# Softmax sums of a cross-attention: their reciprocals sent through memory and fetched back for all partitions, in place of a matrix product

## The chip, the cores and the metric

The kernel runs on one core of one Trainium2 chip. The metric is the device time of one execution in microseconds; the times shown are the median and the extremes of three runs. The profile is of one further execution.

## What is computed

The reference is one layer on x of shape (4, 256, 256), with a context of shape (4, 4096, 256): cross-attention, then a block that sends the top quarter of the tokens through a small attention and the rest through a state-space scan, then a mixture of eight experts. The change concerns the cross-attention:

```
q1 = split_heads(x1 @ Wq1)            # x1 = layernorm(x): 4 batches, 256 tokens, 8 heads of 64
k  = concat(x1 @ Wk1, ctx @ Wk2)      # 256 + 4096 = 4352 keys
v  = concat(x1 @ Wv1, ctx @ Wv2)
sim  = einsum('bihd,bjhd->bhij', q1, k) * 64 ** -0.5
attn = softmax(sim, axis=-1)
out  = einsum('bhij,bjhd->bihd', attn, v)
x = x + out.reshape(B, 256, 512) @ Wo + bo
```

The kernel leaves the probabilities unnormalised, sums them, and multiplies the output of each head and query by the reciprocal of its sum.

## The kernel before

**Tiling.** Heads go in pairs: a group G is one of 16 pairs of heads (4 batches by 4 pairs). A group's 256 queries are taken in 8 steps of 32 queries, so the stage has 128 steps, n = 8G + s, and two more to drain it. In a step the scores of 32 queries with all 4352 keys stand in PSUM (`su`), with four quarters of the keys on the four quarters of the partitions, once for each of the two heads. VectorE copies them to SBUF with their maximum (`copy_max`, L1401) and multiplies these maxima into `mq` (L1408); TensorE spreads the maxima (`stat`, L1413), and VectorE reduces them to `nb` (L1418). ScalarE takes the exponentials in place and leaves their sums in `ls` (`exps`, L1429). VectorE transposes them in blocks of 32 into `pt` (`turn`, L1438). When four steps are there, TensorE multiplies them with the values (`values`, L1447), in four pieces of a step with s = 1 or s = 5, into a PSUM tile `po`, which ScalarE copies to `ao` (`values_out`, L1484). Keys and values are made from the context, chunk by chunk, in the other steps (`k_chunk` L1328, `v_chunk` L1365).

**The sums of a group.** In the first step of the next group (s = 0), `sums(G - 1)` brings together the four quarters by a small product with `dm` (L1461), takes the reciprocals (`rl`, 64 partitions by 8 steps, L1466) and lays them out on diagonals (`dg`, L1468). In the step after it (s = 1), `spread(G - 1)` multiplies `dg` with the constant `pair` (L1475): in `psr`, a PSUM tile of 128 partitions by 256 queries, every partition then holds the reciprocals of its head. `normalize` (L1490) multiplies the two halves of `ao` with it, the first half in the middle of that step, the second one at its end, after `values_out` and the two transposes of the step.

**PSUM.** All short-lived products share the three banks of the pool `ps_m`: `bank(name)` takes one. `po` holds one through a step with s = 1, and `psr` another, from its product to the second `normalize`.

**Order.** The program is written out in order by hand. Between the pieces of a step, `slot(budget)` lets background generators issue the next piece of their work: the router, the small attention and the state-space scan of the batch before (`routed`, `attention`, `ssm_front`, `ssm_scan`). A planner's count `now[0]` grows by what each piece of TensorE work should take; a background piece is issued when its due time has come and its cost fits the budget. In the scan, `make` issues the decays (`da`, ScalarE, L731) and inputs (`db`, GpSimd, L736), `scan` the recurrence (VectorE, L743), and `output` the products (GpSimd, L749 and L751). Background transfers leave from SyncE's queue; small results also leave from ScalarE's. In the front of the background there are the tiles `pspr`, `projT`, `psas`, `psdt`, `ev` and `psat` (L556, L560, L419, L579, L586, L437), all of which but `projT` and `ev` are banks of `ps_m`. `bb` and `cb` (L714) are the scan's inputs, broadcast to all partitions from `bcd` in memory.

A last stage after the 130 steps computes the experts and the background of the last batch.

Of the kernel before, what the change touches and what calls it, by code (L numbers as in the profile page):

```python
# [8 lines left out]
F32 = mybir.dt.float32  # L9
AF = mybir.ActivationFunctionType  # L10
ALU = mybir.AluOpType
# [3 lines left out]
P = 128  # L15
B, T, D = 4, 256, 256
# [21 lines left out]
def bc(ap, axis, n):  # L38

    ap = ap.unsqueeze(axis)  # L40
    shape = list(ap.shape)
    shape[axis] = n
    return ap.to_broadcast(shape)
# [3 lines left out]
def perceiver_layer(ctx: ExitStack, tc: tile.TileContext, a: dict, out: bass.AP):  # L47
# [174 lines left out]
    def bank(name):  # L222
        return ps_m.tile([P, 512], F32, tag="m", name=name)
# [981 lines left out]
    with ExitStack() as s1:  # L1205
# [83 lines left out]
        def turn_x(b):  # L1289
# [9 lines left out]

        su = ps_s.tile([P, 5 * 512], F32, name="su")  # L1300


        pair = fin.tile([2 * 32, P], F32, name="pair")
        nc.vector.tensor_copy(
            pair.rearrange("p (j d) -> p j d", j=2), bc(quarter[: 2 * 32, 0:2, 0], 2, HD)
        )
        qzs = [fin.tile([P, 2, T], F32, name=f"qz{i}") for i in range(2)]
        for t in qzs:
            nc.gpsimd.memset(t, 0.0)
# [141 lines left out]
                        start=(k == 0), stop=(k == NJ - 1),  # L1451
                    )

        dgs, rss = {}, {}

        def sums(G):

            b, hp = divmod(G, NHP)
            ps = bank("psl")
            for j in range(2):  # L1460
                nc.tensor.matmul(  # L1461
                    ps[j * 32 : (j + 1) * 32, :8], dm, lss[b][:, hp, :, j],
                    start=True, stop=True,
                )
            rl = fin.tile([2 * 32, 8], F32, tag="rl", name="rl")
            nc.vector.reciprocal(rl, ps[: 2 * 32, :8])  # L1466
            dgs[G] = fin.tile([2 * 32, 8, 32], F32, tag="dg", name="dg")
            nc.vector.tensor_tensor(  # L1468
                dgs[G], bc(rl, 2, 32), bc(dm[: 2 * 32, :], 1, 8), ALU.mult
            )  # L1470

        def spread(G):

            rss[G] = bank("psr")[:, :T]
            nc.tensor.matmul(  # L1475
                rss[G], pair, dgs[G].rearrange("p s i -> p (s i)"), start=True, stop=True
            )

        def values_out(m):
# [39 lines left out]
        with tc.manual_schedule():  # L1519
            norms = {}  # L1520
            k_chunk(0, 0)
            wself[0] = load_self(0)
            nc.scalar.dma_start(out=bo_bc, in_=a["xbo"].partition_broadcast(P))
            for _ in norm(0):
                pass
            for g in range(1, NCH):
                k_chunk(0, g)
                if g == 4:
                    turn_x(0)
            k_self(0)  # L1530
            start(load_later())
            wv[0] = load_v(0)
            N = 8 * NG
            for n in range(N + 2):
                G, s = divmod(n, 8)
                new, old = n < N, 1 <= n <= N


                pieces, took = [], 1.75
                if s == 5 and G + 1 < NG:  # L1540
                    wv[G + 1] = load_v(G + 1)
                if s % 4 == 1:
                    m, took = n // 4 - 1, 1.95
                    if m >= 0:
                        pieces = [
                            lambda i=i: values(m, i, min(i + 9, NJ)) for i in range(0, NJ, 9)
                        ]
                elif 2 <= s <= 4 and G < NG:
                    pieces = [
                        lambda g=g: v_chunk(G, g) for g in range(3 * s - 6, 3 * s - 3)  # L1550
                    ]
                elif G + 1 < NG:
                    if s == 0:
                        wqk[G + 1] = load_qk(G + 1)
                        wself[G + 1] = load_self(G + 1)
                    pieces = {
                        0: [lambda g=g: k_chunk(G + 1, g) for g in range(3)],
                        6: [lambda g=g: k_chunk(G + 1, g) for g in range(3, 6)],
                        7: [lambda: k_self(G + 1)]
                        + [lambda g=g: k_chunk(G + 1, g) for g in range(6, 8)],  # L1560
                    }[s]


                tail = n >= N - 2

                def piece(i):
                    if i < len(pieces):
                        pieces[i]()
                    if i < len(pieces) or tail:
                        now[0] += took  # L1570

                if new:
                    scores(n)
                    now[0] += 2.1
                if old:
                    exps(n - 1)
                if new:
                    copy_max(n)
                piece(0)
                if s % 4 != 1:  # L1580
                    slot(1.3)
                    piece(1)
                    if old:
                        turn(n - 1, 0)
                    if new:
                        stat(n)
                        now[0] += 0.3
                    if s == 0 and n:
                        sums(G - 1)
                        now[0] += 0.2  # L1590
                    if old:
                        turn(n - 1, 1)
                    slot(1.3 if tail else 0.5)
                    piece(2)
                    slot(2.9)
                else:
                    last = s == 1 and G
                    if last:
                        spread(G - 1)
                        now[0] += 0.6  # L1600
                    slot(1.5)
                    piece(1)
                    if new:
                        stat(n)
                        now[0] += 0.3
                    slot(2.8)
                    if last:
                        normalize(m - 1)
                    if n == N + 1:

                        psx[B - 1] = bank("psx")
                        project(B - 1, 0, psx[B - 1], range(NHP))
                        add(B - 1, 0, psx[B - 1])
                        project(B - 1, 1, psx[B - 1], range(NHP - 1))
                    piece(2)
                    slot(1.5)
                    piece(3)
                    if n > 4:
                        values_out(m)
                    if old:  # L1620
                        turn(n - 1, 0)
                        turn(n - 1, 1)
                    if last:
                        normalize(m)
                        if m % 8 == 7:
                            start_first(finish_batch(m // 8))
                b = n // 32 + 1
                if b < B:
                    if n % 32 == 20:
                        norms[b] = norm(b)  # L1630
                    if n % 32 in (20, 22):
                        next(norms[b])
                    if n % 32 == 29:
                        turn_x(b)
# [301 lines left out]
```

## Time and profile before

| | us |
|---|---|
| median of 3 runs | 1546.52 |
| lowest, highest | 1540.41, 1550.73 |
| profiled execution, own time | 1548.97 |
| its span (first to last instruction) | 1547.3 |
| TensorE busy | 1458.9 (94%) |
| VectorE busy | 1059.8 (68%) |
| ScalarE busy | 757.8 (49%) |
| GpSimd busy | 410.6 (27%) |

The attention stage fills the first 1273 us of the span. In the profile, PE is TensorE, PEld its weight loads, DVE VectorE, ACT ScalarE, POOL GpSimd and SP SyncE; L and a number is a line of the kernel. Lines of the timeline give the start and the duration in us, the engine, the line, the operation, the tile written and those read, and in brackets how long the engine was idle before it and what it waited for. Groups of one tile give lowest, median and highest duration in ns, and the first and last start in us. A product of 32-bit floats shows as two passes, each with its weight load, so the counts of TensorE are doubled. Rows of DMA issues give the number, the size and the median time from issue to landing.

### The profile page before, as it was taken

The page shows a single profiled execution, that of the slowest core. Times are in us where ns is not written, and L with a number is a line of the kernel's source. Part 1 is how long each engine was busy: PE and PEld are TensorE (multiplying, and loading weights), DVE is VectorE, ACT ScalarE, POOL GpSimd, SP SyncE. Part 2 cuts the span into 40 slices and gives each one's busy share as a digit, 9 for nine tenths or more (in the row PEclk, how much of TensorE's full clock was granted, in tenths as well). Part 3 has the DMA queues.
Part 4 walks back from the last instruction along what each step waited for, and adds up shares of the span by engine and source line. Part 5 has one row for each costly group of instructions (what it writes and reads, how often), then busy time and mean ns, then how long its engine had stood idle before and what let it go on. Part 6 is the DMA issues. An engine that isn't in the chain of part 4 may idle for free.

```text
span 1547.3 us, 37278 instructions
## 1 busy us (share of the span) xinstructions
PE 1458.9 (94%) x15686; PEld 1039.8 (67%) x15686; DVE 1059.8 (68%) x1825; ACT 757.8 (49%) x1485; POOL 410.6 (27%) x464
## 2 busy tenths in 40 slices
PE   7999999999999999999999999999998968889799
PEld 3757667576666576775766666758575658778687
DVE  1666666666599976565899866757999554589553
ACT  3444454455566745454666453656654413544211
POOL 1000000000079950000599600003998010110100
PEclk9999999999999999999999999999999979999999
DMA  7455433514245434333554434244452206678471
GB/s 233 135 155 161 157 126 125 174 63 155 95 145 168 161 109 153 119 102 111 162 164 131 144 127 150 68 156 133 141 171 91 74 27 213 208 258 270 157 231 48
DMA packets 157768, 223.41 MB, mean 144 GB/s; under 512 B 14977, under 2 KB 76161, under 8 KB 157601
## 3 DMA queue, kind: packets, MB, share of 16 engines
q1 hardware_dynamic: 152368, 211.45, 42.1%
q10 hardware_dynamic: 3744, 5.51, 1.2%
q0 software_dynamic: 1488, 4.07, 0.9%
q8 instruction: 124, 2.03, 0.5%
q14 instruction: 44, 0.35, 0.1%
HBM read 216.56 MB, written 4.42 MB: 143 GB/s over the span
## 4 chain that ended last, share of the span: by engine, by line
PE 64%; POOL 15%; DVE 10%; DMA 4%; issue 4%; ACT 2%; SPq 0%; ACTq 0%; DVEq 0%; POOLq 0%
PE po L1447 12%; PE su L1381 11%; PE psv L1365 11%; PE psk L1328 9%; POOL y L751 5%; POOL db L736 5%; POOL db L749 5%; DVE sp L1401 3%; PE su L1389 2%; PE pg L1853 2%; PE pu L1853 2%; PE pde L1866 2%; PE p1b L1721 2%; DMA gateT<-in_gateT 2%; DVE db L743 1%
## 5 line engine op out<-in xcount | busy, mean ns | idle before, releaser
L1401 DVE TENSOR_SCALAR_CACHE_REDUCE sp<-su 128x1088 f32<-128x1088 f32 x256 | 318.8, 1281 | 182.0 <-PE su L1389 181.8
L1438 DVE STREAM_TRANSPOSE pt<-sp 128x1088 f32<-128x1088 f32 x256 | 328.0, 1295 | 58.7 <-PE po L1447 58.7
L1429 ACT ACTIVATE sp<-sp,nb 128x1088 f32<-128x1088 f32 x256 | 305.2, 1195 | 13.5 <-DVE nb L1418 13.3
L1447 PE MATMUL po<-pt,v 128*64 128x128 f32 x4352 | 262.9, 278 | 2.3 <-DVE pt L1438 1.3
L1381 PE MATMUL su<-kt,qz 64*32 64x512 f32 x4096 | 256.3, 609 | 4.4 <-DVE nb L1418 3.7
L1328 PE MATMUL psk<-ctx,wk 128*128 128x512 f32 x512 | 244.3, 611 | 10.5 <-DMA ctx<-in_ctxT 7.4
L1365 PE MATMUL psv<-wv,ctx 128*128 128x128 f32 x2048 | 250.8, 279 | 0.2 <-ACT da L731 0.2
L1447 PEld LDWEIGHTS po<-pt,v 128*64 128x64 f32 x4352 | 240.9, 139 | 13.9 <-issue 7.5
L1365 PEld LDWEIGHTS psv<-wv,ctx 128*128 128x128 f32 x2048 | 236.6, 192 | 6.4 <-issue 1.3
L1328 PEld LDWEIGHTS psk<-ctx,wk 128*128 128x128 f32 x512 | 91.3, 191 | 94.8 <-issue 84.4
L1316 ACT COPY kt<-psk 128x512 f32<-128x512 f32 x128 | 74.6, 584 | 158.2 <-PE psk L1328 157.9
L1381 PEld LDWEIGHTS su<-kt,qz 64*32 64x32 f32 x4096 | 63.4, 108 | 123.8 <-issue 94.6
L751 POOL TENSOR_TENSOR y<-y,db 128x192 f32<-128x192 f32 x192 | 135.2, 704 | 15.0
L1369 ACT COPY v<-psv 128x512 f32<-128x512 f32 x144 | 79.1, 557 | 120.0 <-PE psv L1365 118.7
L743 DVE TENSOR_TENSOR_SCAN db<-da,db 128x384 f32<-128x384 f32 x96 | 122.5, 1276 | 14.4 <-POOL db L736 3.7
L395 POOL TENSOR_TENSOR kbd<-qk,hmask 128x512 f32<-128x512 f32 x8 | 8.2, 1042 | 413.2 <-ACT qk L385 413.2
L749 POOL TENSOR_TENSOR db<-db,cb 128x384 f32<-128x384 f32 x96 | 111.1, 1157 | 24.3 <-DVE da L741 24.3
L736 POOL TENSOR_TENSOR db<-bb,xc 128x384 f32<-128x384 f32 x96 | 110.9, 1176 | 0.2
L1389 PEld LDWEIGHTS su<-kt,qz 128*32 128x32 f32 x2048 | 34.6, 109 | 109.4 <-issue 109.4
L731 ACT ACTIVATE da<-delta,A_log_sb 128x192 f32<-128x192 f32 x192 | 75.6, 447 | 51.9 <-DVE da L741 39.0
L1484 ACT COPY ao<-po 128x128 f32<-128x128 f32 x32 | 8.4, 263 | 150.6 <-PE po L1447 150.6
L1413 PEld LDWEIGHTS su<-mq,same 128*128 128x128 f32 x256 | 41.3, 193 | 54.7 <-DVE mq L1408 37.9
(298 smaller groups left out, 1589.5 us busy)
## 6 DMA issues: line engine op xcount, KB each, us to landing
ctx<-in_ctxT SPq DMA_DIRECT2D x256, 512.0 KB, 4.8
gateT<-in_gateT SPq DMA_DIRECT2D x27, 512.0 KB, 4.6
upT<-in_upT SPq DMA_DIRECT2D x27, 512.0 KB, 5.6
downT<-in_downT SPq DMA_DIRECT2D x27, 512.0 KB, 6.5
bb<-bcd SPq DMA_DIRECT2D x24, 192.0 KB, 4.3
cb<-bcd SPq DMA_DIRECT2D x24, 192.0 KB, 3.6
wv<-in_wv SPq DMA_DIRECT2D x32, 128.0 KB, 2.3
in_w<-in_in_w SPq DMA_DIRECT2D x32, 128.0 KB, 3.7
```

Of the source, the lines that this page charges most:

```text
L736: nc.gpsimd.tensor_tensor(db, bbs[k], bc(xc[:, m, :], 1, SG), ALU.mult)
L743: nc.vector.tensor_tensor_scan(out=db, data0=da, data1=db, initial=0.0, op0=ALU.mult, op1=ALU.add,)
L749: nc.gpsimd.tensor_tensor(db, db, cbs[k], ALU.mult)
L751: nc.gpsimd.tensor_tensor(y[:, m, :], y[:, m, :], db[:, s, :], ALU.add)
L1328: nc.tensor.matmul(ps, wqk[G][:, 0, c, :], ct[:, c, :], start=(c == 0), stop=(c == KD - 1),)
L1365: nc.tensor.matmul(ps[:, i * P : (i + 1) * P], lhsT, wv[G][:, w, c, :], start=(c == 0), stop=(c == KD - 1),)
L1369: nc.scalar.copy(v.rearrange("p k d -> p (k d)"), ps[:, : n * P])
L1381: nc.tensor.matmul(su[q * 32 : (q + 1) * 32, SC[j] + lo : SC[j] + lo + 512], qT[r, j, s * 32 : (s + 1) * 32], kt[r, q, lo : lo + 512], sta ...
L1401: nc.vector.tensor_scalar(out=sps[n][j], in0=su[:, SU[j] : SU[j] + QK], scalar1=1.0, scalar2=None, op0=ALU.mult, op1=ALU.max, accum_out=nm ...
L1429: nc.scalar.activation(sps[n][j], sps[n][j], AF.Exp, bias=nbs[n][:, j : j + 1], accum_out=lss[b][:, hp, s, j : j + 1],)
L1438: nc.vector.transpose(pts[m, j][:, i, :], sps[n][j])
L1447: nc.tensor.matmul(pos[m][j * HD : (j + 1) * HD, :], vts[m // 2, k // 4][:, k % 4, j * HD : (j + 1) * HD], pts[m, j][:, :, kk * 32 : (kk + ...
```

## The change

`dg`, `pair` and the product are gone. `sums` writes the reciprocals into one of two tiles of 64 by 32 that were cleared at the start, and VectorE transposes it in blocks of 32: row s of the blocks then holds the 32 reciprocals of step s. `spread`, now issued in the step s = 0 behind the third piece of that step, sends 8 rows of 128 bytes for each of the two heads to a tile in memory, in two transfers from ScalarE's queue. `fetch`, issued in the step s = 1 after its first slot, reads them back from ScalarE's queue into a tile `rs` in SBUF, each head's 256 values to 64 partitions. `normalize` is unchanged in text and reads `rs`. The planner's count no longer grows by 0.6 at that place.

```diff
-        pair = fin.tile([2 * 32, P], F32, name="pair")
-        nc.vector.tensor_copy(
-            pair.rearrange("p (j d) -> p j d", j=2), bc(quarter[: 2 * 32, 0:2, 0], 2, HD)
-        )
...
-        dgs, rss = {}, {}
+        rts, rds, rss = {}, {}, {}
+        rls = [fin.tile([2 * 32, 32], F32, name=f"rl{i}") for i in range(2)]
+        for t in rls:
+            nc.gpsimd.memset(t, 0.0)
 
         def sums(G):
...
-            rl = fin.tile([2 * 32, 8], F32, tag="rl", name="rl")
-            nc.vector.reciprocal(rl, ps[: 2 * 32, :8])
-            dgs[G] = fin.tile([2 * 32, 8, 32], F32, tag="dg", name="dg")
-            nc.vector.tensor_tensor(
-                dgs[G], bc(rl, 2, 32), bc(dm[: 2 * 32, :], 1, 8), ALU.mult
-            )
+            rl = rls[G % 2]
+            nc.vector.reciprocal(rl[:, :8], ps[: 2 * 32, :8])
+            rts[G] = fin.tile([2 * 32, 32], F32, tag="rt", name="rt")
+            nc.vector.transpose(rts[G], rl)
 
         def spread(G):
 
-            rss[G] = bank("psr")[:, :T]
-            nc.tensor.matmul(
-                rss[G], pair, dgs[G].rearrange("p s i -> p (s i)"), start=True, stop=True
+            rd = dram.tile([2, 8, 32], F32, tag="rd", name="rd")
+            for j in range(2):
+                nc.scalar.dma_start(out=rd[j], in_=rts[G][j * 32 : j * 32 + 8, :])
+            rds[G] = rd
+
+        def fetch(G):
+            rss[G] = fin.tile([P, T], F32, tag="rs", name="rs")
+            nc.scalar.dma_start(
+                out=rss[G],
+                in_=rds[G].rearrange("j s i -> j (s i)").unsqueeze(1).to_broadcast([2, HD, T]),
             )
...
                     slot(1.3 if tail else 0.5)
                     piece(2)
+                    if s == 0 and n:
+                        spread(G - 1)
                     slot(2.9)
                 else:
                     last = s == 1 and G
+                    slot(1.5)
                     if last:
-                        spread(G - 1)
-                        now[0] += 0.6
-                    slot(1.5)
+                        fetch(G - 1)
                     piece(1)
```

## The prediction, made before the changed kernel had run

> **What bounds the kernel now.** I read the page first: engine shares, slices, chain.
>
> ```profile
> PE 1458.9 (94%) x15686; PEld 1039.8 (67%) x15686; DVE 1059.8 (68%) x1825; ACT 757.8 (49%) x1485; POOL 410.6 (27%) x464
> ...
> PE   7999999999999999999999999999998968889799
> ...
> DVE  1666666666599976565899866757999554589553
> ...
> PE 64%; POOL 15%; DVE 10%; DMA 4%; issue 4%; ACT 2%; SPq 0%; ACTq 0%; DVEq 0%; POOLq 0%
> ```
>
> TensorE is busy nearly throughout and holds 64% of the chain. VectorE is at 9 tenths only in three stretches (slices 11 to 13, 20 to 22, 28 to 30): there the background runs a batch's state-space scan, and TensorE and VectorE take turns as the bound. So each of the 16 places the change touches, one per head pair, has to be read in its own stage. Next, the answers for the removed tiles, `psr` and `dg`:
>
> ```profile
> L1475 PEld LDWEIGHTS psr<-dg,pair x32: 182/184/187, 106.3 to 1263.3; 64*128 64x128 f32 x32
> L1475 PE MATMUL psr<-dg,pair x32: 376/428/481, 106.4 to 1263.5; 64*128 64x256 f32 x32
> L1468 DVE TENSOR_TENSOR dg<-rl,same x16: 416/418/753, 100.5 to 1258.0; 64x256 f32<-64x256 f32 x16
> ```
>
> Each product is two passes. The third view is the timeline around these products. They fall into four kinds. **Quiet** (six: 106, 175, 243, 312, 628, 947 us): no heavy background.
>
> ```profile
> 109.60 0.28 DVE L1490 TENSOR_TENSOR ao<-ao,psr 128x128 f32<-128x128 f32 x1
> ...
> 113.23 2.50 DVE L1438 STREAM_TRANSPOSE pt<-sp 128x1088 f32<-128x1088 f32 x2 [3.35 <-PE po L1447]
> ```
>
> After the first normalising multiply VectorE stands idle 3.35 us until TensorE's values are done. **Front** (three: 397, 714, 1033), the background's attention and state-space front:
>
> ```profile
> 1032.79 0.70 PE L1475 MATMUL psr<-dg,pair 64*128 64x256 f32 x2
> 1033.41 1.50 PE L556 MATMUL pspr<-xc,xproj_w_sb 128*48 128x192 f32 x8
> ...
> 1035.40 1.08 PE L419 MATMUL psas<-kbd,qk 128*64 128x512 f32 x4 [0.49 <-ACT projT L560]
> ...
> 1041.66 0.91 PE L579 MATMUL psdt<-projT,dt_w 16*128 16x192 f32 x4
> ...
> 1044.01 1.09 PE L437 MATMUL psat<-ident,pa 128*128 128x128 f32 x4 [1.44 <-ACT ev L586]
> ```
>
> Neither wait is for data: `psas` doesn't read `projT`, `psat` doesn't read `ev`. Both wait for a PSUM bank. Of the three of pool `ps_m`, `po` holds one and `psr` another, from its product to the last multiply of the step, so the background is left with one. **Scan, second step** (three: 477, 793, 1112):
>
> ```profile
> 1112.15 0.70 PE L1475 MATMUL psr<-dg,pair 64*128 64x256 f32 x2
> ...
> 1114.85 1.62 DVE L743 TENSOR_TENSOR_SCAN db<-da,db 128x384 f32<-128x384 f32 x1
> ...
> 1116.56 0.80 ACT L731 ACTIVATE da<-delta,A_log_sb 128x192 f32<-128x192 f32 x2 [2.78 <-DVE da L741]
> ...
> 1118.79 0.26 DVE L1490 TENSOR_TENSOR ao<-ao,psr 128x128 f32<-128x128 f32 x1
> ...
> 1124.17 0.44 DVE L1408 TENSOR_TENSOR mq<-nm,quarter 128x8 f32<-128x8 f32 x1
> ...
> 1124.77 0.29 PE L1413 MATMUL su<-mq,same 128*128 128x8 f32 x2
> ```
>
> VectorE has no gap from the multiply on; its `mq` ends at 1124.61 and TensorE's statistic starts at 1124.77, so the two engines are level. **Scan, last step** (three: 550, 866, 1183) has no decays left on ScalarE. One more is the end of the stage (1263).
>
> [...] `mq` (two SBUF inputs) takes 0.17 us in quiet steps and 0.44 to 0.68 in the scan, `dg` 0.42 and 0.75, while the multiply, whose second input is in PSUM, takes 0.25 to 0.29 everywhere.
>
> **Part by part.**
>
> *Product removed.* In the timeline the next TensorE work starts 0.62 us after the product does (1112.15 to 1112.77). Quiet steps are bound by TensorE: 6 x 0.62 = 3.7 us.
>
> *Bank freed.* In each front step 0.49 and 1.44 us of bank wait go. Next in line are data: `pa`'s exponentials, ready at 1038.67, long before `psat`; and the activations of the first `psdt`, which follow `zs` and so move earlier by the same amount. 3 x (0.62 + 0.49 + 1.44) = 7.6 us.
>
> *VectorE: `dg` becomes a 64x32 transpose.* The 128x1088 transpose takes 1.295 us, 1.2 ns a column; 32 columns with the overhead of small operations, 0.1 to 0.15. Saved: 0.3 us in quiet steps (covered by TensorE), 0.6 in the scan. Per step the two multiplies now have both inputs in SBUF: [...]in the scan like `mq`, about 0.35 more each.
>
> *Two writes, ScalarE's queue, step s = 0.* 2 x 0.33 us of issue (the `bcd<-projT` row's instruction), 8 rows of 128 B each. They stand behind the copy of the third key chunk, which waits for TensorE; the transpose is done before that (`dg` ended at 1107.51, the copy began at 1107.90), so no wait is added. Behind them the exponentials move by at most 0.3 us, while the transposes that need these wait for `po`. Cost 0.
>
> *The fetch, ScalarE's queue, step s = 1.* Its issue waits for the writes, sent a step (about 8 us) earlier: landed. What counts is its position and its flight time L. In the records of single packets a 1,024 B packet takes 46 ns (median); 64 in a row are 2.9 us. Small loads land in 1.7 us (`dt_w`) and 192 KB broadcasts in 3.0 at least:
>
> ```profile
> bb<-bcd SPq DMA_DIRECT2D x24, 192.0 KB, 4.3
> ...
> bcd<-projT ACTq DMA_DIRECT2D x4, 24.0 KB, 1.4
> ```
>
> 1.7 + 2.9 = 4.6 is the lower end on two engines; reading one row 64 times has stretched the broadcast packets (1,536 B: 65 ns median, 99 mean), which gives 1.7 + 64 x 0.066 = 5.9. I take L = 5.0. On sixteen engines it would be about 3.0.
>
> Quiet: issued after the exponentials at about 105, landed by 110 to 111; the transposes behind the waiting multiply start at about 112.6. Hidden. Front: behind `pa`'s exponentials (1037.0 when moved), landed at 1042; VectorE's next urgent work is after 1045. Hidden. Scan, last step: issued after the exponentials at about 1183.7, 5.6 us before the multiply; just hidden. **Scan, second step**: a decay of the first slot stands ahead of it, waiting for the scan of 1114.85. With VectorE 0.65 earlier that scan ends at 1115.82, the fetch goes out at about 1116.1 and lands at 1121.1; the multiply is due at 1118.14. VectorE stops for 3.0 us, and behind it wait both transposes, the second multiply, the next copies of the scores and `mq`, and for `mq` TensorE. VectorE's balance: -0.65 + 3.0 + 0.7 = +3.05, less 0.16 of margin: about 2.9 us lost, 3 x 2.9 = 8.6.
>
> *Scan, last step.* 0.3 saved each: VectorE's dearer multiply eats half of the 0.62: 0.9. *End*: writes land at about 1260, the fetch at 1265, where `psx` would start at 1265.3: 0.2 kept.
>
> *Planner.* The count gains 0.6 less per head pair. Background pieces that fell in the slot just after it were overdue by 2.4 or more, and later due times are relative, so I leave the order as it is; one idle poll at n = 129 moves. Start-up: `pair` (0.21 us) goes, two small memsets come on an idle GpSimd; 0.
>
> Sum: 3.7 + 7.6 + 0.9 + 0.2 - 8.6 = 3.8 us saved. The profiled execution took 1548.97 us (span 1547.3 and 1.7 around it), giving 1545.2; it is 2.5 above the median of the runs, 1546.52, so 1542.7 for a median: I say 1543.
>
> **Rivals.** *A: the fetch spreads over sixteen engines.* For it: every other 128-partition load of the trace does. [...] Then L = 3.0; the stall is 1.0, VectorE's balance -0.65 + 1.0 + 0.7 - 0.16 = +0.9, and 12.4 - 2.7 = 9.7 us are saved: about 1537. *B: the fetch is late (slower).* For it: broadcast reads of `bcd` took up to 7.1 us. Each us of L past 2.1 costs 3 us in the second scan steps, past 5.6 three more in the last ones; the 12.4 gained elsewhere are used up at L = 5.9 (3 x 3.8 + 3 x 0.3). At L = 7.1 the loss is 12.4 - 15 - 4.5 = 7 us over before: about 1554. At 8.5 it is 15. *C: the bank stays short*, if the pool hands the background the bank just released: then 5.8 of the front's gain go and the kernel is 2 us slower, 1548. Against: key chunks follow each other with no gap, so banks rotate.
>
> **Chances.** Forecast 0.48, A 0.17, B 0.25, C 0.10. Likeliest: 1543. Own range of the forecast (L from 4.6 to 5.6): 1541 to 1545. To hold 8 in 10 it reaches past A and B, plus the 5 us by which medians of three may differ: 1530 to 1556. A change of 1% (15.5 us) is about what measurements of this kernel can tell from none: faster 0.13 (A and gains unseen), slower 0.08 (B past 8.5 us), same 0.79.
>
> **What would show it.** The groups `psr` and `pair` are gone; `psat` no longer waits for `ev`; the fetch's row in the DMA issues shows 128 KB and L; in the steps at 477, 793 and 1112 the multiply L1490 waits about 3 us for a DMA and `mq` after it holds up the statistic L1413. L near 3 means A, 5.9 or more B. Wrong altogether if the multiply waits in the quiet steps too, or if the writes hold up ScalarE.

## The result and the profile after

| | before | after |
|---|---|---|
| median of 20 runs each, us | 1547.37 | 1541.03 |
| lowest, highest | 1540.41, 1552.11 | 1533.95, 1551.43 |
| profiled execution, us | 1548.97 | 1543.37 |
| its span | 1547.3 | 1541.7 |

The ratio is 0.9962, with a 95% interval from 0.9949 to 0.9975: the change saves 4 to 8 us, about 0.4%. The forecast was 1543 us, 3.8 us saved, with a change of more than 1% unlikely. The page after, engine shares and shares of the chain:

```profile
PE 1450.0 (94%) x15654; PEld 1038.0 (67%) x15654; DVE 1064.2 (69%) x1824; ACT 758.9 (49%) x1485; POOL 401.6 (26%) x466
...
PE 60%; DVE 18%; POOL 9%; issue 5%; DMA 5%; ACT 2%; SPq 0%; ACTq 0%; DVEq 0%; POOLq 0%
```

TensorE is 8.9 us less busy, yet its span is only 5.6 us shorter, and VectorE's share of the chain has gone from 10% to 18%. VectorE's total has risen although the 8.1 us of `dg` are gone. The groups say where (total busy time, mean ns, then idle time before and its releaser). The multiply, first of the kernel before, then of the kernel after with the rows that matter beside it:

```profile
L1490 DVE TENSOR_TENSOR ao<-ao,psr 128x128 f32<-128x128 f32 x32 | 8.4, 261 | 8.4 <-ACT ao L1484 5.6 <-PE psr L1475 2.8
```

```profile
L1408 PE MATMUL su<-mq,same 128*128 128x8 f32 x256 | 43.6, 242 | 34.1 <-DVE mq L1403 29.5 <-DVE da L741 4.5
L1495 DVE TENSOR_TENSOR ao<-ao,rs 128x128 f32<-128x128 f32 x32 | 13.9, 435 | 39.5 <-DMA rs<-rd 30.3 <-ACT ao L1489 5.6 <-issue 3.6
L1466 DVE STREAM_TRANSPOSE rt<-rl 64x32 f32<-64x32 f32 x16 | 3.3, 203 | 0.6
L437 PEld LDWEIGHTS psat<-ident,pa 128*128 128x128 f32 x16 | 1.7, 140 | 0.7 <-issue 0.7
```

The multiply takes 435 ns on average in place of 261 and waits 30.3 us for the fetch. TensorE's statistic waits 29.5 us for `mq`; before, it was 20.0. The wait of `psat` for `ev`, 5.2 us on the weight loads of the three fronts, is gone.

The timelines after, one of each kind of place. Quiet, the first of the six (writes issued at 102.91, fetch at 110.03, multiply 4.9 us later; the transposes start at once because `po` is done by then, but at 115.11 where the kernel before had them at 113.23):

```profile
102.91 1.18 ACTq L1474 DMA_DIRECT2D rd<-rt  x2
...
110.03 0.61 ACTq L1479 DMA_DIRECT2D rs<-rd  x1
...
114.90 0.29 DVE L1495 TENSOR_TENSOR ao<-ao,rs 128x128 f32<-128x128 f32 x1 [5.24 <-DMA rs<-rd]
115.11 2.50 DVE L1433 STREAM_TRANSPOSE pt<-sp 128x1088 f32<-128x1088 f32 x2
```

Front (`psas` and `psat` follow their predecessors with no wait for another engine):

```profile
1030.00 1.02 PE L419 MATMUL psas<-kbd,qk 128*64 128x512 f32 x3
...
1036.19 0.91 PE L579 MATMUL psdt<-projT,dt_w 16*128 16x192 f32 x4
...
1037.03 0.66 PE L437 MATMUL psat<-ident,pa 128*128 128x128 f32 x4
```

Scan, second step (the fetch leaves behind a decay, the first multiply waits for it, and in the end TensorE waits for `mq`):

```profile
1107.78 0.52 ACTq L1479 DMA_DIRECT2D rs<-rd  x1
...
1112.16 1.01 DVE L1495 TENSOR_TENSOR ao<-ao,rs 128x128 f32<-128x128 f32 x1 [2.25 <-DMA rs<-rd]
...
1115.52 0.30 DVE L1495 TENSOR_TENSOR ao<-ao,rs 128x128 f32<-128x128 f32 x1
...
1118.27 0.38 DVE L1403 TENSOR_TENSOR mq<-nm,quarter 128x8 f32<-128x8 f32 x1
...
1118.70 0.39 PE L1408 MATMUL su<-mq,same 128*128 128x8 f32 x2 [2.86 <-DVE mq L1403]
```

Scan, last step (no wait for the fetch, which left 8.65 us ahead, but both multiplies are long; GpSimd's instruction ahead of the first one is shown too):

```profile
1174.29 0.51 ACTq L1479 DMA_DIRECT2D rs<-rd  x1
...
1182.16 1.65 POOL L749 TENSOR_TENSOR db<-db,cb 128x384 f32<-128x384 f32 x1
1182.94 1.03 DVE L1495 TENSOR_TENSOR ao<-ao,rs 128x128 f32<-128x128 f32 x1
...
1186.31 0.64 DVE L1495 TENSOR_TENSOR ao<-ao,rs 128x128 f32<-128x128 f32 x1
```

To see which of the places gave what (all but the end of the stage), I took for every step the time from its first score product to that of the next step, and subtracted the kernel before (us, profile against profile; a step's delay often shows in the step after it, so s = 1 and s = 2 are added). The table also has the experiments below.

| kernel | quiet | front | scan, second | scan, last |
|---|---|---|---|---|
| predicted | -0.62 | -2.55 | +2.9 | -0.3 |
| after | -0.78 | -4.5, -4.6, -4.6 | +3.4, +4.2, +3.6 | +0.40, +0.40, +0.25 |
| again_after | -0.78 | -4.5, -4.6, -4.6 | +4.4, +2.6, +3.5 | +0.41, +0.41, +0.26 |
| again_before | 0 | -1.55, 0, 0 | 0 | 0, 0, +1.2 |
| e_16 | -0.78 | as after | +1.4, +1.3, +1.2 | +0.41, +0.40, +0.23 |
| e_early | -0.78 | as after | +1.3, +1.3, +1.3 | +0.39, +0.42, +0.26 |
| e_early16 | -0.78 | as after | +1.3, +1.3, +1.2 | +0.40, +0.41, +0.24 |
| e_nodma | -0.78 | as after | +1.0, +1.2, +1.3 | +0.36, +0.40, +0.23 |
| e_bank | -0.78 | -2.3, -2.4, -2.4 | +2.5, +2.6, +2.6 | +0.37, +0.38, +0.22 |
| e_copy | 0 | -3.8, -3.8, -3.8 | +1.7, +1.7, +1.4 | +0.68, +0.67, +0.80 |
| e_direct | -0.78 | as after | +0.2, +0.3, +0.3 | -0.21, -0.21, -0.03 |

The quiet column holds for five of the six quiet places. The first, at 106 us, is another matter: +0.84 us after, +0.41 in again_after, +0.30 in e_early and +1.05 in e_bank, all with the fetch on two engines (e_16, below); -0.76 to -0.78 in e_16, e_early16 and e_nodma, where it is spread over more engines or left out. There the flight of the fetch isn't hidden. It leaves ScalarE's queue 3.4 us after the last exponential, because it waits for the two writes, whose last packet ended only at 109.46. The order of the background's instructions on ScalarE and GpSimd is the same before and after, so the smaller count of the planner moved nothing there.

### The profile page after: what moved, and what is told of

The parts are those of the page before. It is cut to its first block, busy times and chain, and to the rows that moved or that the text cites. A ratio compares the mean times of both kernels' runs of the same rounds, so it can differ in the third digit from the quotient of the medians.

```text
span 1541.7 us, 37326 instructions
## 1 busy us (share of the span) xinstructions
PE 1450.0 (94%) x15654; PEld 1038.0 (67%) x15654; DVE 1064.2 (69%) x1824; ACT 758.9 (49%) x1485; POOL 401.6 (26%) x466
## 4 chain that ended last, share of the span: by engine, by line
PE 60%; DVE 18%; POOL 9%; issue 5%; DMA 5%; ACT 2%; SPq 0%; ACTq 0%; DVEq 0%; POOLq 0%
PE psv L1360 10%; PE su L1376 10%; PE po L1442 10%; PE psk L1323 9%; DVE sp L1396 6%; DVE db L743 4%; POOL y L751 3%; DVE pt L1433 3%; POOL db L736 3%; POOL db L749 3%; PE su L1384 2%; PE pg L1859 2%; PE pde L1872 2%; PE pu L1859 2%; PE p1b L1727 2%
## 5 line engine op out<-in xcount | busy, mean ns | idle before, releaser
L1396 DVE TENSOR_SCALAR_CACHE_REDUCE sp<-su 128x1088 f32<-128x1088 f32 x256 | 318.8, 1282 | 186.2 <-PE su L1384 186.2
L1442 PE MATMUL po<-pt,v 128*64 128x128 f32 x4352 | 258.6, 276 | 2.1 <-DVE pt L1433 1.3
L1360 PE MATMUL psv<-wv,ctx 128*128 128x128 f32 x2048 | 254.1, 281 | 0.0
L751 POOL TENSOR_TENSOR y<-y,db 128x192 f32<-128x192 f32 x192 | 139.8, 728 | 15.0
L743 DVE TENSOR_TENSOR_SCAN db<-da,db 128x384 f32<-128x384 f32 x96 | 126.5, 1317 | 11.4 <-POOL y L751 0.5
L731 ACT ACTIVATE da<-delta,A_log_sb 128x192 f32<-128x192 f32 x192 | 75.5, 447 | 49.8 <-DVE da L741 30.3
L736 POOL TENSOR_TENSOR db<-bb,xc 128x384 f32<-128x384 f32 x96 | 99.6, 1060 | 0.2
```

Of the source, the lines that this page charges most:

```text
L736: nc.gpsimd.tensor_tensor(db, bbs[k], bc(xc[:, m, :], 1, SG), ALU.mult)
L743: nc.vector.tensor_tensor_scan(out=db, data0=da, data1=db, initial=0.0, op0=ALU.mult, op1=ALU.add,)
L751: nc.gpsimd.tensor_tensor(y[:, m, :], y[:, m, :], db[:, s, :], ALU.add)
L1360: nc.tensor.matmul(ps[:, i * P : (i + 1) * P], lhsT, wv[G][:, w, c, :], start=(c == 0), stop=(c == KD - 1),)
L1396: nc.vector.tensor_scalar(out=sps[n][j], in0=su[:, SU[j] : SU[j] + QK], scalar1=1.0, scalar2=None, op0=ALU.mult, op1=ALU.max, accum_out=nm ...
L1442: nc.tensor.matmul(pos[m][j * HD : (j + 1) * HD, :], vts[m // 2, k // 4][:, k % 4, j * HD : (j + 1) * HD], pts[m, j][:, :, kk * 32 : (kk + ...
```

## Experiments

Each ratio is to the kernel before, run beside the experiment on the same chip; the kernel before took from 1546.7 to 1550.1 us there, so times of different chips are compared by their ratios.

### Sixteen engines (e_16)

```diff
         def fetch(G):
             rss[G] = fin.tile([P, T], F32, tag="rs", name="rs")
-            nc.scalar.dma_start(
-                out=rss[G],
-                in_=rds[G].rearrange("j s i -> j (s i)").unsqueeze(1).to_broadcast([2, HD, T]),
-            )
+            for j in range(2):
+                nc.scalar.dma_start(
+                    out=rss[G][j * HD : (j + 1) * HD, :],
+                    in_=rds[G][j].rearrange("s i -> (s i)").partition_broadcast(HD),
+                )
```

> Edit: the fetch as two transfers, one for each head[...], at the same place. Theory 1 (two engines make the flight long): the 128 packets spread over sixteen engines, flight falls from 4.4-4.9 us to about 2.5-3.0 us; VectorE's wait for the fetch in the scan's second steps falls from 2.3-5.2 us to 1 us or less, the TensorE clock is no longer halved there, and these three groups cost 0 to 1 us each against the kernel before in place of 2.3-4.8: about 1531 to 1535 us. Theory 2 (the flight is latency and the crowd of the scan's own transfers, not the number of engines): flight stays over 4 us, time stays at 1540 to 1543 us. Either way the second issue costs ScalarE 0.5 us a group.

1531.89 us, ratio 0.9917 (0.9886 to 0.9948). The packets of ScalarE's queue show the engines (packets, MB, share of 16 engines). After, then e_16:

```profile
q10 hardware_dynamic: 6336, 7.64, 1.5%
```

```profile
q10 hardware_dynamic: 6816, 7.64, 1.6%
```

The timeline of e_16 in the scan's second step:

```profile
1099.74 0.46 ACTq L1480 DMA_DIRECT2D rs<-rd  x1
1100.30 0.55 ACTq L1480 DMA_DIRECT2D rs<-rd  x1
...
1102.91 0.64 DVE L1496 TENSOR_TENSOR ao<-ao,rs 128x128 f32<-128x128 f32 x1 [0.99 <-DMA rs<-rd]
...
1105.90 0.27 DVE L1496 TENSOR_TENSOR ao<-ao,rs 128x128 f32<-128x128 f32 x1
...
1108.62 0.72 DVE L1403 TENSOR_TENSOR mq<-nm,quarter 128x8 f32<-128x8 f32 x1
```

The bytes are the same, and 480 packets are more: 30 for each of the 16 fetches. In the packet records of after, each fetch has 128 packets of 1,024 bytes and two of 4 bytes. The first packet starts 1.3 us after the issue, and the 128 take 2.7 us in most groups; added up they are 5.9 us, so about two are under way at a time, with 43 ns for each of 64 in a row. Two transfers of `x4d` on the same queue (128 KB each, issued from 584.94 on) have 256 such packets and 32 of 4 bytes, and their 12.3 us fall into 1.6: 7.7 at a time. In the trace of before, the 25 transfers of this queue have 400 packets of 4 bytes, sixteen each on average. Sixteen packets of 4 bytes for each of the two transfers of e_16 in place of two for the one fetch are the 30 more. So I read the fetch of the changed kernel as one on two engines, and that of e_16 as one on sixteen; the first rests on the overlap of the packets, the second on the counts alone. From issue to landing it is 4.0 to 4.7 us after. In e_16 it is 2.7 to 3.2 us in the scan's second steps and the fronts, and up to 4.5 in other places. VectorE's wait falls from 2.25 to 0.99 us in the step shown, and the steps lose 1.3 us in place of 3.4 to 4.2. Theory 1 holds, with a little more left than the 0 to 1 us it gave; theory 2 falls.

### Early fetch (e_early), and both (e_early16)

```diff
                     last = s == 1 and G
-                    slot(1.5)
                     if last:
                         fetch(G - 1)
+                    slot(1.5)
```

> Edit: the same fetch (two engines), issued ahead of the slot of step s = 1 instead of behind it, so that no decay stands before it in ScalarE's queue. Theory 1 (the stall of the scan's second steps is the queue position plus the flight): the fetch goes out about 3 us earlier, at the end of the exponentials, and lands before the multiply is due; no wait of VectorE for it in those steps, 3 x 4 us less than the changed kernel: about 1530 to 1533 us. Theory 2 (the early fetch waits for the writes and holds up ScalarE, so the decays come later): VectorE's scan starves instead, 1540 us or more, with a wait of da for the DMA.

> Both edits. Theory 1: each of the two takes the stall away alone, so both together bring no more than the better one, 1529 to 1533 us; what is left against the kernel before in the scan's last steps (+0.3 us a group, the multiply with two inputs in SBUF beside GpSimd) stays. Theory 2 (the two are independent costs): both together save 3 us or more over the better one alone.

e_early: 1534.11 us, 0.9922 (0.9897 to 0.9947). e_early16: 1532.25 us, 0.9916 (0.9896 to 0.9936), and once more, beside e_direct, 1533.82, 0.9915 (0.9895 to 0.9936). The timeline of e_early:

```profile
1103.29 0.52 ACTq L1479 DMA_DIRECT2D rs<-rd  x1
...
1106.95 1.66 POOL L749 TENSOR_TENSOR db<-db,cb 128x384 f32<-128x384 f32 x1
1108.15 0.60 DVE L1495 TENSOR_TENSOR ao<-ao,rs 128x128 f32<-128x128 f32 x1 [0.35 <-DMA rs<-rd]
...
1109.92 1.96 POOL L736 TENSOR_TENSOR db<-bb,xc 128x384 f32<-128x384 f32 x2
1111.10 0.93 DVE L1495 TENSOR_TENSOR ao<-ao,rs 128x128 f32<-128x128 f32 x1
...
1114.48 0.72 DVE L1403 TENSOR_TENSOR mq<-nm,quarter 128x8 f32<-128x8 f32 x1
```

In the scan the slow fetch, sent ahead of the decays, costs no more than the fast one sent behind them: the stall was position plus flight, and taking away most of either is enough. All three are alike within their intervals, some 6 to 7 us below the changed kernel by the ratios (0.9962 less 0.9915 to 0.9922). But none of them brings the step back to the level of the kernel before: +1.3 us stay.

### No transfers at all (e_nodma)

```diff
+        one = fin.tile([P, T], F32, name="one")
+        nc.gpsimd.memset(one, 1.0)
...
         def spread(G):
-            rd = dram.tile([2, 8, 32], F32, tag="rd", name="rd")
-            for j in range(2):
-                nc.scalar.dma_start(out=rd[j], in_=rts[G][j * 32 : j * 32 + 8, :])
-            rds[G] = rd
+            return
...
         def fetch(G):
-            rss[G] = fin.tile([P, T], F32, tag="rs", name="rs")
...
+            rss[G] = one
```

> Edit, on the kernel with the early fetch over sixteen engines: no writes and no fetch; normalize multiplies with a tile of ones in SBUF that was set at the start, so the division by the sums is left out. Theory 1 (with the early, spread fetch the round trip through memory is hidden everywhere): within 2 us of that kernel, 1530 to 1533 us. Theory 2 (the writes, issues and fetch still cost ScalarE and the queues something, 16 x 0.2 to 0.5 us): 1524 to 1528 us.

1532.56 us; its ratio of 0.9886 (0.9849 to 0.9923) covers that of e_early16. Place by place it is as e_early16 too (table). So with an early fetch over sixteen engines the trip through memory costs nothing that shows, and the +1.3 us are not the fetch. In the groups the multiply is now at its dearest, with no transfer to wait for:

```profile
L1491 DVE TENSOR_TENSOR ao<-ao,one 128x128 f32<-128x128 f32 x32 | 16.1, 502 | 5.6 <-ACT ao L1485 5.6
```

### The product kept, its result copied out (e_copy)

```diff
-            rss[G] = bank("psr")[:, :T]
+            ps = bank("psr")[:, :T]
...
+            rss[G] = fin.tile([P, T], F32, tag="rs", name="rs")
+            nc.scalar.copy(rss[G], ps)
```

> Edit, on the kernel before: ScalarE copies psr to a tile in SBUF right after the product, and normalize reads that; the product and dg stay, nothing goes through memory. Theory 1 (the front's gain is the bank, the scan's loss beyond the fetch is the multiply's two SBUF inputs): in the fronts psas and psat no longer wait for projT and ev, 2.2 us less each (3.7 where the clock is not halved there either); quiet steps unchanged; the scan's second and last groups lose about 1 us each through the multiply and 0.2 through ScalarE's copy; total 3 x 2.2 to 3 x 3.7 less 6 x 1.1: 1542 to 1547 us. Theory 2 (the multiply's inputs don't matter): 1535 to 1540 us.

1546.61 us, with 1550.14 for the kernel before on that chip: 0.9976 (0.9963 to 0.9990), as theory 1 says. In quiet steps, with the product back, the gain of 0.78 is gone. In the fronts `psat` follows at once, as after. In the scan both multiplies are long although nothing comes from memory. The timeline:

```profile
1039.14 0.66 PE L437 MATMUL psat<-ident,pa 128*128 128x128 f32 x4
...
1113.68 1.03 DVE L1492 TENSOR_TENSOR ao<-ao,rs 128x128 f32<-128x128 f32 x1
1117.06 0.94 DVE L1492 TENSOR_TENSOR ao<-ao,rs 128x128 f32<-128x128 f32 x1
```

### A bank held (e_bank)

```diff
                 else:
                     last = s == 1 and G
+                    if last:
+                        held = bank("psr")
+                        nc.vector.memset(held[:, :1], 0.0)
                     slot(1.5)
...
                     if last:
                         normalize(m)
+                        junk = fin.tile([P, 1], F32, tag="jk", name="jk")
+                        nc.vector.tensor_copy(junk, held[:, :1])
```

> Edit: the changed kernel, with a PSUM bank of ps_m held from the place of the old product to the second multiply (one column set by VectorE at the start, read by VectorE at the end; its content isn't used). Theory 1 (the front's gain is the freed bank): psas waits again for projT and psat for ev, the TensorE clock is halved again for 3.4 us at the three fronts, and 3 x 3.5 to 4 us come back: about 1552 to 1556 us, of which up to 1.5 us are the two small VectorE instructions. Theory 2 (the gain is the product's own time and the order around it): the fronts keep their -4.5 us, time within 2 us of the changed kernel, 1541 to 1545 us.

1545.57 us, 0.9989 (0.9971 to 1.0007): by the medians slower than the changed kernel, though the two intervals just overlap, and by less than expected. The places decide it. The waits (sum in us, times, longest) and the timeline show that the bank's waits came back in full:

```profile
PEld psat L437 <- ACT ev L586: 5.2, 3, 1.7
```

```profile
1031.28 1.08 PE L419 MATMUL psas<-kbd,qk 128*64 128x512 f32 x4 [0.49 <-ACT projT L560]
...
1039.89 0.66 PE L437 MATMUL psat<-ident,pa 128*128 128x128 f32 x4 [1.44 <-ACT ev L586]
```

Each front is 2.23 us longer than after (-2.3 against -4.5), the two waits and 0.3 more. The halved clock, which I had expected to return with the wait, did not. That leaves 4.54 - 2.23 - 0.78 = 1.5 us of each front to be explained.

### The two kernels profiled once more (again_before, again_after)

> The kernel before, unchanged, profiled once more. Theory 1[...]: the waits at the three fronts are there again, 1.4 us each, but the halved stretches fall elsewhere or stay away; where they stay away, the front step is 1.5 us shorter than in the first profile, in all three alike. Theory 2 (the wait itself halves the clock[...]): the three stretches of 3.4 us return, right at the wait for ev.

> The changed kernel, unchanged, profiled once more. Theory 1[...]: VectorE's wait for the fetch in the scan's second steps returns at 2.3 to 3 us each, the halved stretches may fall elsewhere; where they stay away, steps s = 1 and 2 there cost 2.5 us against the kernel before in place of 3.4 to 4.2. Theory 2: they return in all three.

Spans of 1547.3 and 1539.6 us. Windows around the first front of the kernel before (start and end, length, busy time of PE, PEld, DVE, ACT and POOL, then the share of its full clock that TensorE was granted, DMA share and GB/s), in the first profile:

```profile
407.00:411.00 4.00, 2.56 (x22) 2.10 (x22) 0.00 (x0) 1.94 (x5) 0.00 (x0) 0.77 0.00 0
411.00:415.00 4.00, 4.00 (x66) 2.15 (x63) 2.40 (x2) 2.35 (x4) 0.00 (x0) 0.80 0.00 0
```

In the second profile the wait for `ev` is the same, by the timeline and then the windows:

```profile
407.29 0.65 PE L437 MATMUL psat<-ident,pa 128*128 128x128 f32 x4 [1.45 <-ACT ev L586]
```

```profile
406.00:410.00 4.00, 2.71 (x40) 2.11 (x48) 0.34 (x1) 2.13 (x7) 0.00 (x0) 1.00 0.00 0
410.00:414.00 4.00, 4.00 (x68) 2.67 (x52) 4.00 (x6) 2.46 (x5) 0.00 (x0) 1.00 0.00 0
```

In the first profile the clock is halved for 3.41 us after this wait (0.77 and 0.80 are means over 4 us), in the second it stays at 1.00, and the step is 1.55 us shorter. At the other two fronts of the second profile it is halved again. After, against this undisturbed front, is -4.54 + 1.55 = -2.99 us, which is the product's 0.78 and the bank's 2.23; the -3.8 of e_copy are the bank's 2.23 and the clock's 1.55. The scan's second steps of the kernel after show the same. The middle one (at 798 us), first profile and second:

```profile
798.00:802.00 4.00, 1.51 (x14) 1.32 (x12) 3.96 (x8) 0.94 (x2) 3.69 (x6) 1.00 0.65 143
802.00:806.00 4.00, 3.63 (x18) 3.64 (x18) 3.78 (x7) 0.00 (x0) 2.25 (x4) 0.57 0.80 302
```

```profile
798.00:802.00 4.00, 2.08 (x19) 1.88 (x17) 4.00 (x6) 1.17 (x2) 3.77 (x6) 1.00 0.63 78
802.00:806.00 4.00, 3.06 (x34) 2.42 (x42) 3.86 (x8) 0.59 (x1) 2.71 (x4) 1.00 0.98 369
```

TensorE waits 2.85 and 2.86 us for `mq` in the two; with the halved clock the step loses 4.2 us, without it 2.6, as in e_bank. So neither theory is right as it stood: theory 1 had the three fronts alike, theory 2 the halved clock at each of the waits. The halved stretch returned at two fronts of three and at two of the three scan steps, and in e_bank, with the same waits, at none of the three fronts. What decides is left open (last section).

### The multiply with fewer SBUF inputs (e_onein, e_direct)

e_onein:

```diff
-            nc.vector.tensor_tensor(ao, ao, rss[G][:, q], ALU.mult)
+            nc.vector.tensor_scalar(
+                out=ao, in0=ao, scalar1=rss[G][:, half : half + 1], scalar2=None, op0=ALU.mult
+            )
```

> Edit, on the kernel with the early fetch over sixteen engines: normalize multiplies each half of ao with one column of rs (a scalar for each partition) in place of its 128 columns, so that the instruction has one SBUF input besides the scalar; the values are then those of one query for all. Theory 1 (what is left of the loss in the scan is the multiply's contention with GpSimd): the multiply takes 0.25-0.35 us in the scan too, in place of 0.6-1.0, and the steps s = 1 and 2 of the scan's second and last groups lose 1.0 us less each, 6 x 1.0 = 6 us: about 1525 to 1527 us. Theory 2 (what is left is the order of VectorE's work, not the length of the multiply): 1530 to 1533 us, as with two inputs.

1530.25 us, 0.9863 (0.9832 to 0.9894), with intervals that overlap those of e_nodma and e_direct beside it. The edit did not do what it was meant to: in the scan the instruction is as long as before, so the run doesn't tell the theories apart. The timeline of a scan's second step:

```profile
1102.74 0.96 DVE L1496 TENSOR_SCALAR ao<-ao,rs 128x128 f32<-128x128 f32 x1
...
1106.05 0.93 DVE L1496 TENSOR_SCALAR ao<-ao,rs 128x128 f32<-128x128 f32 x1
```

At the fronts, with GpSimd idle, it takes 0.24 to 0.28 us. So beside GpSimd the `tensor_scalar`, with one SBUF input of 128 columns and one of a single column, is as long as the multiply with two full ones. e_direct, again on the kernel with the early fetch over sixteen engines, has the input in PSUM instead:

```diff
-                    if n > 4:
+                    if last:
+                        ao = aos[divmod(G - 1, NHP)][:, P:]
+                        nc.vector.tensor_tensor(ao, pos[m], rss[G - 1][:, P:], ALU.mult)
+                    elif n > 4:
                         values_out(m)
                     if old:
                         turn(n - 1, 0)
                         turn(n - 1, 1)
-                    if last:
-                        normalize(m)
```

> Edit, on the kernel with the early fetch over sixteen engines: for the second half of a group, ScalarE's copy of po to ao and the multiply of ao become one multiply of VectorE that reads po in PSUM and rs in SBUF, ahead of the step's transposes; the first half is as it was. Theory 1 (contention needs two SBUF inputs): this multiply takes 0.25-0.3 us in the scan, the second half's excess of 0.4-0.7 us goes in six steps: 2 to 4 us less than that kernel, 1528 to 1530 us. Theory 2 (the multiply ahead of the transposes holds them back by its wait for po, which they wait for anyway, and po's bank is held no longer than before): no change beyond 1 us in the quiet steps either way. Slower than 1533 would mean that holding po for VectorE costs more than the copy.

> The kernel with the early fetch over sixteen engines, timed beside the next one on the same chip: 0.988 to 0.992 of the kernel before, 12 to 18 us less, 4 to 8 us below what the changed kernel has.

> The kernel with the second half multiplied straight from PSUM, timed beside the one above. If the shorter multiply counts, it is 2 to 4 us below that kernel; if the time comes back later in the scan, as the steps s = 4 of its first profile say (+0.5 us there), within 1.5 us of it.

First 1531.93 us, 0.9860 (0.9828 to 0.9893); then beside e_early16 1531.19, 0.9890 (0.9868 to 0.9912), where that has 1533.82, 0.9915 (0.9895 to 0.9936). The two halves by the groups, the first with two inputs in SBUF, the second with one in PSUM:

```profile
L1496 DVE TENSOR_TENSOR ao<-ao,rs 128x128 f32<-128x128 f32 x16 | 9.1, 567 | 4.9 <-DMA rs<-rd 4.9
L1627 DVE TENSOR_TENSOR ao<-po,rs 128x128 f32<-128x128 f32 x16 | 4.6, 288 | 33.7 <-PE po L1442 33.7
```

And in a scan's second step, by the timeline:

```profile
1103.45 1.03 DVE L1496 TENSOR_TENSOR ao<-ao,rs 128x128 f32<-128x128 f32 x1
1104.41 0.28 DVE L1627 TENSOR_TENSOR ao<-po,rs 128x128 f32<-128x128 f32 x1
```

The second half takes 278 to 293 ns in all 16 groups, the scan's included. In the scan it starts within 0.02 us of the start of a GpSimd instruction, so by itself it doesn't show what happens in the middle of one. The kernel before does: its multiply of 1118.79, 0.26 us long with an input in PSUM, lies inside this instruction:

```profile
1118.02 1.66 POOL L749 TENSOR_TENSOR db<-db,cb 128x384 f32<-128x384 f32 x1
```

Together they show that the multiply is held up beside GpSimd when both its inputs are in SBUF (0.93 to 1.03 us in the scan's second steps of e_nodma) and not when one is in PSUM (0.25 to 0.29). The scan's second steps lose 0.2 to 0.3 us in place of 1.3, the last ones gain 0.2 in place of losing 0.4. But part comes back: in the steps s = 3 and 4 of the groups of the second steps, e_early16 loses 0.6 us together and e_direct 1.2. The medians differ by 2.6 us, and the intervals of the two overlap; whether e_direct is the faster of the two is not settled. Both beat both kernels.

## Why the prediction was right, and where it was not

**Bound and places.** Right in the main: the kinds of place behave as said, but for the first quiet one and the scan's last steps, and the largest single loss sits at 477, 793 and 1112 us with the multiply waiting for the fetch and the statistic for `mq`.

**Product.** Right in kind; the term was 0.62 us and measured 0.78 in quiet steps. e_copy, which keeps the product with `dg` and the planner's count, shows 0 there, so it goes with the product. I had taken the distance from its start to the next TensorE work, which is 0.16 too little.

**Bank.** Right: e_bank gives back the waits for `projT` and `ev`, 2.23 us a front where I had 0.49 + 1.44 = 1.93. **Not seen:** the halved clock behind that wait. In the profile of before it stood at all three fronts and cost 1.5 us each, so the front's term of -2.55 measured -4.5 to -4.6.

**Writes and quiet steps.** The prediction took the writes for landed, a step of about 8 us ahead of the fetch. That holds at the fronts and in the scan's second steps (7.8 to 8.3 us). In the quiet steps they leave only 3.4 to 6.5 us ahead, and the fetch goes out about 0.6 us after their last packet. So VectorE's multiply waits for it in all six quiet steps (1.4 to 5.2 us) and at the three fronts (2.8 to 3.6), which the prediction had named as a sign of being wrong altogether. The sign was too strong: VectorE would have stood waiting for `po` there anyway, and at five of the six places the step gains its 0.78 as without any transfer. At the first it loses 0.4 to 0.8.

**Fetch.** Two engines were my assumption, which no trace of before showed; the packet records after do, with about two packets of a fetch under way at a time (e_16). L, to the multiply, was 4.4 to 4.9 us, once 5.2, where VectorE was not late itself; I took 5.0 from a range whose lower end of 4.6 was nearer. Rival A, sixteen engines, is ruled out; rival B, a slow fetch, too, since L stayed under 5.9; rival C, the bank short as before, is refuted by the missing wait of `psat`.

**Stall in the scan's second steps.** +2.9 predicted, +2.6 measured without the halved clock (again_after, e_bank) and 3.4 to 4.4 with it. The sum was nearly right, but its terms were not. I had 3.0 for the stall and 0.7 less 0.65 for the rest of VectorE's balance. Measured, 1.3 stay without any transfer, and the stall adds only about 1.3, though VectorE stands for 2.25. The timelines tell why. From the first score product for s = 2, which is sent ahead of the multiply, to the end of its `mq` it takes 8.9 us after (1109.76 to 1118.65) and 7.5 in e_early (1107.66 to 1115.20). The multiply starts 1.9 us later after, and is 0.4 us longer; but the second one takes 0.30 us in place of 0.93 and `mq` 0.38 in place of 0.72, because VectorE, being late, meets GpSimd at another point: the second multiply starts 0.15 us before the end of the GpSimd instruction then running, in e_early 0.78 before it. 1.9 + 0.4 - 0.6 - 0.3 = 1.4. Stall and contention don't add up.

**Scan, last steps.** The step that failed outright: -0.3 predicted, +0.25 to +0.40 measured. The fetch was hidden, as said. The multiply's price was the error: 0.35 us dearer each, taken from `mq`; it was 0.77 and 0.39 in the last of them (1.03 and 0.64 against 0.26 and 0.25), and 1.03 and 0.93 us were seen in e_copy's and e_nodma's second steps, where no transfer shifts them. The price is not one of the instruction: both `mq` and the multiply end a fixed short time after the GpSimd instruction that runs when they start (last section), so they cost what is left of that. In the timeline above the first multiply starts 0.78 us into an instruction of 1.65 and ends 0.15 behind it. `mq` itself took from 0.29 to 0.82 us beside GpSimd in the kernel before, not only the 0.44 to 0.68 that were read.

**The rest.** The transpose was 203 ns, not 100 to 150; its place is covered. The writes cost nothing that e_nodma would have won back from e_early16. The 0.2 us at the end of the stage is not singled out by these runs. Sum without the clock: 6 x 0.78 + 3 x 3.0 - 3 x 2.6 - 3 x 0.35 = 4.8 us, or 3.2 to 3.6 with the first quiet place as measured (+0.4 to +0.8), where the prediction had 3.8; the runs say 4 to 8. What the other steps gained or lost is not in it. The effects of the clock stand on both sides, 3 x 1.5 gone at the fronts and up to 1.8 come at each second scan step. That the medians agree so well is in part luck: it rests on errors that offset each other. Gains were put too small by 0.45 at each front and 0.16 in five quiet steps, too large by 0.65 in each of the scan's last steps and by 1.0 to 1.5 in the first quiet one.

## What to carry to other kernels

A result that VectorE read beside a working GpSimd was dearer in SBUF than in PSUM where the other operand was in SBUF too (up to 1.04 us in place of 0.25 to 0.29): price the reader, not only the product that goes, and price it by what is left of GpSimd's instruction when the reader starts. The small fetch through memory cost nothing that shows once it was issued ahead of the decays and spread over sixteen engines (e_early16 is as e_nodma place by place), so look for what can block the queue ahead of such a fetch; in the scan's second steps moving it up by one slot (+1.3 us left) was worth as much as spreading it over sixteen engines (+1.2 to +1.4). A fetch of what was just written also waited for the writes: in the quiet steps it left about 0.6 us after their last packet. And when two profiles are compared, look at the granted clock behind each wait before a step's whole difference is put down to the edit.

## What the runs showed of the hardware

**The clock behind a short wait.** Every halved stretch of these profiles, but for the last that the trace's end cuts, lasts 3.41 us or a multiple of it. In the first profile of the kernel before, so do the stretches at full clock between them: 47.38 to 409.20 us is 106 times 3.413, 412.61 to 726.64 is 92 times. So the changes of the clock in one execution fall on a grid of 3.413 us, whose cells are called windows here. A wait of 1.45 us was followed by a halved window at five fronts (three before, two in again_before). It fell each time into one window, in which TensorE was busy for 58% of the time by the records. At the undisturbed front of again_before it was split over two windows (78% and 80%). That would suggest that the wait must fall into one window, and the scan's waits of 2.85 us for `mq` fit: after five windows that TensorE was busy for 16 to 43% (after, again_after) a halved one came, and where the wait was split, with 50% or more busy in each part (once in again_after, three times in e_bank), none. But the waits at e_bank's three fronts fell into one window each, of 58 or 59%, and none was halved after it. So neither the share of busy time nor the window alone tells; what does, these runs don't show. In the first profile of the kernel before the three waits for `ev` end 316.5 and 318.8 us apart, close to 93 windows (317.4), so in one execution they can be hit alike; what is the luck of one execution then looks like an effect in three places.

The scatter between executions goes with the clock too: over 15 runs of the kernel before, taken beside e_16, span and mean granted clock have a correlation of -0.90, with 1.1 us for each thousandth of the clock.

**Contention by what GpSimd has left.** A VectorE multiply of 128x128 with both inputs in SBUF took 0.25 to 0.29 us with GpSimd idle and up to 1.04 beside it. In the eleven profiles that have it, 119 such multiplies began while a GpSimd `tensor_tensor` ran, with up to 0.89 us of that left. All but two of them ended 0.14 to 0.16 us after the GpSimd instruction did; the two began within 0.12 us of its end and took 0.25 and 0.29 us. `mq`, 8 columns wide, ended 0.02 to 0.03 us after it in all 35 cases of the kernel before, and the `tensor_scalar` of e_onein 0.08 to 0.09. So VectorE's instruction waits for GpSimd's to end, and its own length sets only the short rest. With an input in PSUM nothing waits: 24 multiplies of the two profiles of the kernel before began under the same instructions and took 0.25 to 0.26 us.
